# A two-layer adaLN transformer on one core: another order of the tail, and an earlier modulate in layer 0

## The chip, the cores and the metric

The kernel runs on 1 core of one Trainium2 chip. The metric is device time in microseconds (us) of one execution. Three executions of the kernel before the change took 626.12, 626.17 and 625.37 us: median 626.12. Durations in this document that belong to single instructions come from the profile of one more execution of the same kernel.

A core has five engines, each with its own instruction stream, run strictly in the order in which the kernel writes it: TensorE (PE in the profile; its weight loads are listed as PEld), VectorE (DVE), ScalarE (ACT), GpSimd (POOL) and SyncE (SP), which here only issues DMAs. Engines wait for one another by semaphores.

## The reference: what is computed

Tokens x of shape 8 x 256 x 128 pass through two layers. Each layer is an attention block and a mixture-of-experts block, each with a layernorm in front that is scaled and shifted by vectors worked out from a condition c, and each added back to x with a gate:

```python
h = _layernorm(x, axis=-1) * (1 + ca) + sa
x = x + ga * attention(h)
h = _layernorm(x, axis=-1) * (1 + cb) + sb
x = x + gb * ffn(h)
```

Layer 0: 16 heads of width 8, causal; then 8 experts with a hidden width of 512, top 2 by softmax, plus a shared expert. Layer 1: 16 heads of width 64, causal; then 16 experts with a hidden width of 64 (silu(x wg) * (x wu), times wd), top 2 by sigmoid, plus a shared expert, plus the block's own input.

## The kernel before the change

All of it is in float32. The 2048 tokens lie in four wide tiles of 512 (x[0] to x[3]; a wide tile is two batches of 256, or four token tiles of 128). The change touches `fast_path` only. (The program ends by reading a flag, `bad`, which sends unusual inputs to another path; with these inputs that path isn't taken.)

From the end of layer 0's first layernorm on, the schedule is manual: each engine's order is exactly the order in which the Python code writes the steps.

**Layer 0's attention** is a loop over 24 units (three per batch, line 1427). Unit n issues, in this order: scores0 (TensorE scores, ScalarE exponentials, GpSimd masks), in every third unit the projections of the next batch (project0, L1101, L1104 and L1106), then the list `early[n]` (filled by `at`), then values0 of unit n-2 (L1162), project_v0, and then the list `ends[n]` (filled by `at_end`). Layernorm of wide tile w is cut into `measure`, `normalise` and `modulate`. `modulate` is four transposes on TensorE (L771) and two VectorE writes of h (L774). Wide tile w is measured at the end of unit 6w-6, normalised in 6w-5, and modulated in 6w-3; the projection in unit 6w-2 is the first to read its h. Also in the lists around there: `finish0` (TensorE y L1198, VectorE t L1200 and x L1201), the second layernorm (`norm0`: statistics L746 and L748, xn0b L762), and `gates0` (L1256 to L1261).

**Layer 1's experts.** Wide tiles 0 to 2 are routed sparsely: their tokens were scattered by expert into `xs` in DRAM, in tiles of 128 rows, and ten groups m = 0 to 9 of four tiles each are worked through by

- `fetch_weights1(m)` (m from 4 on, L1760 and L1764): SyncE reads four expert numbers into registers and issues four DMAs of 128 KB. Each group has a buffer of its own or one that is long free.
- `fetch_rows1(m)` (L1742, L1035): four DMAs of 64 KB from `xs`; called by `turn1(m - 4)`.
- `turn1(m)`: four transposes (L1779), a ScalarE copy to xTs (L1781), and `fetch_rows1(m + 4)`.
- `hidden1(m)`: 16 matmuls (L1790), ScalarE silu (L1795), VectorE product (L1796).
- `project_tiles(m)`: 8 matmuls (L1803), two VectorE copies into `ysb` (L1809; three buffers, each free when its DMA has landed), and the DMA of `ysb` to `ys` in DRAM (L1810, 256 KB).

When all of `ys` has landed, `gather1(j)` for the 12 token tiles fetches each token's two rows back (L1047, 24 indirect DMAs on GpSimd). `combine1(j)` weighs and adds them (ScalarE L1912, VectorE L1913); at each wide tile's end it multiplies by the gate and adds to x (L1916, L1917: on GpSimd for wide tiles 0 and 1, on VectorE for 2) and issues the output. The buffers of its sums are shared with the token tiles of `norms`, two in all, so wide tile 1's combine waits for norms[1]'s last step on GpSimd and wide tile 2's for wide tile 0's.

Wide tile 3 is computed densely: `finish1` of the last batch, the layernorm of that batch (`norms[1][0]` measure, `[1]` normalise, `[2]` modulate, `[3]` tokens and `[4]` add, the last two on GpSimd), the router (`go7`, four steps; `go6` is the same for the batch before), `gate_rows(k)` (a transpose, a VectorE copy gT L1829, and DMAs through DRAM into `gp`, L1830 and L1837), `dense_hidden(p)` for 8 pairs of experts (TensorE L1852, ScalarE silu L1846, VectorE product L1847), `dense_gate(p)` (VectorE, times `gp`, L1857) and `dense_project(p)` (TensorE L1862). `shared_hidden`, `shared_project` and `ffn1_add` do the shared expert of two wide tiles, and the final adds (L1894, L1895). `spread_last` (L1648, L1652) and `reciprocals1` belong to the last batch's attention; `tables` is 18 VectorE instructions that make the gather's indices; `flag` reduces the judgement (L1923), adds it up on TensorE and writes `bad` (L1927).

The order of all this after the attention loop is one written list of some 105 calls (from line 2018). The lines that matter most, with their numbers:

```python
    at_end(n + 3, modulate)                        # 1398, in the loop over w
    fetch_weights1(8)                              # 2030
    fetch_weights1(9)                              # 2031
    hidden1(9)                                     # 2059
    for j in range(TT * LAST): gather1(j)          # 2064
```

Of the kernel before, what the change touches and what calls it, by code (L numbers as in the profile page):

```python
# [17 lines left out]
B, S = 8, 256  # L18
# [539 lines left out]
def fast_path(ctx: ExitStack, tc: tile.TileContext, i: dict, out: bass.AP, bad: bass.AP):  # L558
# [819 lines left out]
    def at_end(n, *steps):  # L1378
        ends.setdefault(n, []).extend(steps)
# [13 lines left out]
    for w in range(1, NW):  # L1393
        measure, normalise, modulate = layernorm_parts(w, md[0], SA, CA, f"0a{w}", ps_ln)
        n = 6 * w - 6
        at_end(n, measure)
        at(n + 1, normalise)
        at_end(n + 3, modulate)
        at_head(n + 2, 1, lambda w=w: add_bias(w))
    for b in range(B - 1):  # L1400
        at_end(3 * b + 4, lambda b=b: normalise0(b))
# [194 lines left out]
    def values1(b, u):  # L1596
        v = st1["v", b, u // 2]
        if u == 0:
            st1["s", b] = pp.tile([P, S], F32, tag="sum", bufs=1, name=f"sum1_{b}")
            st1["ou", b] = lp.tile([P, 2, 4, S], F32, tag="ou", name=f"ou1_{b}")  # L1600
        s = st1["s", b]
        o = pp.tile([P, 2, S], F32, tag="o", bufs=1, name=f"o1_{b}_{u}")
        pts = [st1.pop(("pt", b, 2 * u + m)) for m in range(2)]
        for m in range(2):
            for kb, cols, qs in blocks:
                for n in range(2):
                    nc.tensor.matmul(  # L1607
                        out=o[bass.ts(n, D1), m, qs], lhsT=v[:, kb, bass.ts(4 * (u % 2) + 2 * m + n, D1)],
                        rhs=pts[m][:, n, cols], start=(kb == 0), stop=(kb == 1), skip_group_check=True,
                    )  # L1610

        for kb, cols, qs in blocks:
            for m in range(2):
                for n in range(2):
                    nc.tensor.matmul(  # L1615
                        out=s[bass.ts(2 * n + m, 32), qs], lhsT=on[:, u, :], rhs=pts[m][:, n, cols],
                        start=(kb == 0 and u == 0), stop=(kb == 1 and u == 3), skip_group_check=True,
                    )
        nc.vector.tensor_copy(st1["ou", b][:, :, u, :], o)

    def reciprocals1(b):
        r = st1["r", b] = lp.tile([P, S], F32, tag="r", name=f"r1_{b}")
# [12 lines left out]
        st1["rb", b] = rb  # L1635
        judge(r)
# [138 lines left out]
    def turn1(m):  # L1775
        xT_ps = ps_ln([P, 4, P], f"xT1_{m}")
        xg = sq.pop(("x", m))
        for t in range(4):
            nc.tensor.transpose(xT_ps[:, t, :], xg[:, t, :], ident)  # L1779
        xT = sq["xT", m] = lp.tile([P, 4, P], F32, tag="xT", name=f"xTs1_{m}")  # L1780
        nc.scalar.copy(xT, xT_ps)  # L1781
        if m + 4 < NQ:
            fetch_rows1(m + 4)

    def hidden1(m):
        xT = sq.pop(("xT", m))
# [229 lines left out]
    norms = [norm1((b, 1)) for b in (B - 2, B - 1)]  # L2016
    go6, go7 = (one(route1((b, 1))) for b in (B - 2, B - 1))
    values1(*divmod(N - 1, 4))
    reciprocals1(B - 1)
    turn1(0)  # L2020
    hidden1(0)
    turn1(1)
    turn1(2)
    hidden1(1)
    add()
    project_tiles(0)
    fetch_weights1(7)
    turn1(3)
    project_tiles(1)
    fetch_weights1(8)  # L2030
    fetch_weights1(9)
    hidden1(2)
    turn1(4)
    tables()
    hidden1(3)
    norms[0][0]()
    project_tiles(2)
    turn1(5)
    norms[0][1]()
    hidden1(4)  # L2040
    project_tiles(3)
    turn1(6)
    hidden1(5)
    norms[0][2]()
    project_tiles(4)
    turn1(7)
    hidden1(6)
    hidden1(7)
    norms[0][3]()
    project_tiles(5)  # L2050
    go6()
    turn1(8)
    norms[0][4]()
    project_tiles(6)
    turn1(9)
    go6()
    hidden1(8)
    project_tiles(7)
    hidden1(9)
    go6()  # L2060
    project_tiles(8)
    spread_last()
    project_tiles(9)
    for j in range(TT * LAST): gather1(j)
    shared_hidden(0)
    go6()
    finish1(B - 1)
    norms[1][0]()
    gate_rows(0)
    norms[1][1]()  # L2070
    norms[1][2]()
    norms[1][3]()
    shared_project(0)
    go7()
    shared_hidden(2)
    go7()
    dense_hidden(0)
    go7()
    dense_hidden(1)
    go7()  # L2080
    shared_project(2)
    ffn1_add(0)
    dense_hidden(2)
    dense_hidden(3)
    gate_rows(1)
    ffn1_add(1)
    ffn1_add(2)
    dense_hidden(4)
    dense_hidden(5)
    judge(st1["r", B - 1])  # L2090
    norms[1][4]()
    judged = flag()
    next(judged)
    dense_hidden(6)
    dense_gate(0)
    dense_gate(1)
    dense_hidden(7)
    combine1(0)
    dense_gate(2)
    dense_project(0)  # L2100
    combine1(1)
    dense_project(1)
    dense_gate(3)
    dense_project(2)
    dense_project(3)
    combine1(2)
    combine1(3)
    dense_gate(4)
    combine1(4)
    dense_gate(5)  # L2110
    dense_gate(6)
    dense_project(4)
    combine1(5)
    combine1(6)
    combine1(7)
    dense_gate(7)
    dense_project(5)
    combine1(8)
    combine1(9)
    dense_project(6)  # L2120
    dense_project(7)
    combine1(10)
    combine1(11)
    ffn1_add(LAST)
    next(judged, None)
    nc.sync.dma_start(out=out[:, bass.ts(LAST, TT), :], in_=x[LAST])
    manual.close()
    l1.close()

# [93 lines left out]
```

## Time and profile before

| what | us |
|---|---|
| median of three executions | 626.12 |
| the profiled execution | 627.05 |
| its span | 625.2 |
| TensorE busy over the span | 545.0 (87%) |
| VectorE busy | 351.0 (56%) |
| GpSimd busy | 301.8 (48%) |
| ScalarE busy | 274.5 (44%) |
| granted TensorE clock, mean | 0.942 |

The profiled execution lies 1.85 us above its own span, and 0.93 us above the median of the three. "Busy" on TensorE counts pipelined matmuls with modelled ends. The granted clock is the share of TensorE's full speed that it was given: the same hidden1 group of 16 matmuls takes 1.09 us at 1.00 and 1.98 us at 0.50.

Landmarks of the profiled execution, in us from the start of the span: layer 0's attention runs from about 20 to 130; layer 1's attention ends at 525; groups 0 to 9 run from 526.02 (first transpose) to 565.49 (last matmul of group 9); gathers run from 569.52 to 599.34; the last VectorE instruction ends at 615.2.

### The profile page before, as it was taken

What the parts mean: (1) busy time and instruction counts of PE and PEld (TensorE: products, weight loads), DVE (VectorE), ACT (ScalarE), POOL (GpSimd) and SP (SyncE); (2) the same over time, 40 slices, a digit from 0 to 9 for tenths busy, and PEclk for the clock granted to TensorE, in tenths of its full rate; (3) what the DMA queues carried; (4) which work ended last, traced back from release to release, by engine and by line L of the source; (5) the groups of instructions that cost most, each with busy time, mean ns of one, the idle gap of its engine ahead of it and who ended that gap; (6) DMA issues with size and microseconds to landing.
All of it is one profiled execution on the core that took longest, in us unless ns stands there. A gap on an engine that the chain in (4) does not pass through costs nothing.

```text
span 625.2 us, 11930 instructions
## 1 busy us (share of the span) xinstructions
PE 545.0 (87%) x4391; PEld 386.4 (62%) x4391; DVE 351.0 (56%) x1069; ACT 274.5 (44%) x486; POOL 301.8 (48%) x456
## 2 busy tenths in 40 slices
PE   3699879878899899789999999999999998888960
PEld 3344435445699899656676767657676766665350
DVE  3448897875632222246536556574838384644793
ACT  1476465736145455345534363435353532433230
POOL 7356586857404443238532056543446543104771
PEclk9899797979989999979999999999999999879996
DMA  8999990131239999131030203030303036653541
GB/s 277 339 408 403 389 331 9 38 112 34 62 100 285 313 316 308 36 151 35 19 85 10 61 17 88 30 72 2 78 14 87 14 78 186 172 159 77 115 98 56
DMA packets 52911, 85.41 MB, mean 137 GB/s; under 512 B 6428, under 2 KB 32156, under 8 KB 51692
## 3 DMA queue, kind: packets, MB, share of 16 engines
q1 hardware_dynamic: 44444, 59.77, 30.0%
q0 software_dynamic: 8400, 24.78, 12.8%
q8 instruction: 37, 0.61, 0.4%
q14 instruction: 30, 0.25, 0.1%
HBM read 53.46 MB, written 31.07 MB: 135 GB/s over the span
## 4 chain that ended last, share of the span: by engine, by line
PE 61%; DVE 15%; DMA 7%; POOL 5%; ACT 4%; issue 4%; SPq 1%; DVEq 0%; POOLq 0%; ACTq 0%
PE sc L1585 7%; PE o L1607 6%; PE qp L1554 5%; PE hp L1338 5%; PE yt L1346 5%; PE vp L1567 5%; PE kp L1554 4%; PE y L1660 4%; POOL yg L1047 3%; PE sum L1615 3%; PE sc L1137 3%; PE o L1162 2%; DMA wt<-in_wpk_dram,widx 2%; PE hp L1272 2%; PE qk L1101 1%
## 5 line engine op out<-in xcount | busy, mean ns | idle before, releaser
L812 POOL TENSOR_SCALAR_AFFINE_SELECT pt<-pt 128x256 f32<-128x256 f32 (+1 forms) x176 | 89.3, 533 | 112.1 <-ACT pt L1588 79.6
L1047 POOL DMA_INDIRECT yg<-ys,yidx x56 | 53.9, 962 | 52.1 <-DMA ys<-ysb 33.9
L1588 ACT ACTIVATE pt<-sc 128x768 f32<-128x768 f32 x64 | 48.4, 808 | 25.5 <-PE sc L1585 25.4
L1141 ACT ACTIVATE pt<-sc 128x1024 f32<-128x1024 f32 x48 | 46.5, 1023 | 16.7 <-PE sc L1137 16.3
L1039 POOL DMA_INDIRECT wt<-in_wpk_dram,widx x31 | 29.2, 942 | 50.1 <-PE xT L1329 48.6
L1340 ACT ACTIVATE hst<-hp,wt 128x128 f32<-128x128 f32 x136 | 38.9, 368 | 30.4 <-ACT hst L1340 20.5
L1585 PEld LDWEIGHTS sc<-q,k 64*128 64x128 f32 x512 | 41.6, 187 | 16.4 <-issue 11.5
L1585 PE MATMUL sc<-q,k 64*128 64x256 f32 (+1 forms) x512 | 50.5, 336 | 0.0
L1607 PE MATMUL o<-pt,v 128*64 128x256 f32 (+1 forms) x512 | 48.7, 332 | 1.8 <-POOL pt L812 1.8
L1570 ACT COPY v<-vp 128x512 f32<-128x512 f32 x32 | 18.8, 586 | 67.6 <-PE vp L1567 56.7
L1350 DVE COPY ysb<-yt 128x128 f32<-128x128 f32 x39 | 11.4, 291 | 58.5 <-PE yt L1346 58.5
L1607 PEld LDWEIGHTS o<-pt,v 128*64 128x64 f32 x512 | 31.8, 136 | 19.7 <-POOL pt L812 5.6
L1558 DVE COPY q<-qp 128x512 f32<-128x512 f32 x32 | 22.0, 688 | 38.8 <-PE qp L1554 38.8
L1137 PE MATMUL sc<-qm,k 32*128 32x512 f32 x192 | 37.7, 716 | 5.3 <-ACT pt L1141 4.4
L1338 PE MATMUL hp<-xTs,wt 128*128 128x128 f32 x272 | 36.5, 277 | 3.2 <-DMA wt<-in_wpk_dram,widx 2.4
L1554 PE MATMUL qp<-h,wq 128*128 128x256 f32 x128 | 37.1, 413 | 1.3 <-DVE sh L1299 1.3
L924 POOL DMA_INDIRECT xs<-ht0b,idx x32 | 31.7, 990 | 13.5 <-issue 4.8
L1567 PE MATMUL vp<-wv,h 128*128 128x512 f32 x64 | 36.0, 645 | 1.1 <-DVE q L1558 1.1
L1338 PEld LDWEIGHTS hp<-xTs,wt 128*128 128x128 f32 x272 | 33.0, 192 | 4.7 <-issue 3.3
L1346 PE MATMUL yt<-wt,hst 128*128 128x128 f32 x272 | 35.8, 275 | 0.0
L1558 ACT COPY k<-kp 128x512 f32<-128x512 f32 x32 | 18.8, 588 | 35.7 <-PE kp L1554 35.6
L1554 PE MATMUL kp<-h,wk 128*128 128x256 f32 x128 | 33.7, 387 | 0.0
(296 smaller groups left out, 1138.5 us busy)
## 6 DMA issues: line engine op xcount, KB each, us to landing
xs<-zero SPq DMA_DIRECT2D x1, 12288.0 KB
xs<-zero SPq DMA_DIRECT2D x1, 8192.0 KB
rb<-rd SPq DMA_DIRECT2D x14, 512.0 KB, 6.1
mdb<-mrd SPq DMA_DIRECT2D x2, 2048.0 KB
xg<-xs SPq DMA_DIRECT2D x63, 64.0 KB, 2.0
wt<-in_wpk_dram SPq DMA_DIRECT2D x24, 128.0 KB, 2.1
wst<-in_wpk_dram SPq DMA_DIRECT2D x5, 514.0 KB, 12.6
ys<-ysb SPq DMA_DIRECT2D x10, 256.0 KB, 4.7
```

Source lines behind the costliest of these rows:

```text
L812: nc.gpsimd.affine_select(out=pt, in_=pt, compare_op=ALU.is_ge, fill=0.0, base=0, pattern=[[0, pt.shape[1]], [1, P]], channel_multiplier=-1,)
L1047: nc.gpsimd.indirect_dma_start(out=yg[:, k, :], out_offset=None, in_=self.ys[:, :], in_offset=bass.IndirectOffsetOnAxis(ap=self.yidx[:, j, ...
L1137: nc.tensor.matmul(out=sc[:, n, :].rearrange("p (a q) -> p a q", q=rhs.shape[2]), lhsT=k[r, cols], rhs=rhs, start=True, stop=True,)
L1141: nc.scalar.activation(pt[:, bass.ts(half, 2), :], sc, AF.Exp)
L1338: nc.tensor.matmul(out=hp[:, c, :], lhsT=wt[:, bass.ts(c, P)], rhs=xT, start=True, stop=True)
L1346: nc.tensor.matmul(out=y, lhsT=hs[:, c, :], rhs=wt[:, bass.ds(WF + c * P, P)], start=(c == 0), stop=(c == FC - 1))
L1554: nc.tensor.matmul(out=ps_[:, n, :], lhsT=w1[f"w{what}1"][:, bass.ts(2 * u + n, P)], rhs=hb, start=True, stop=True)
L1558: copy(st1[what, b, u], ps_)
L1567: nc.tensor.matmul(out=vp, lhsT=hb[:, bass.ts(j, P)], rhs=w1["wv1"][:, bass.ts(half, 512)], start=True, stop=True)
L1585: nc.tensor.matmul(out=sc[:, n, cols], lhsT=k[r, m, bass.ts(kb, P)], rhs=q[r, m, qs], start=True, stop=True)
L1588: nc.scalar.activation(pt, sc[:, :, 0:384], AF.Exp, scale=1.0 / math.sqrt(D1))
L1607: nc.tensor.matmul(out=o[bass.ts(n, D1), m, qs], lhsT=v[:, kb, bass.ts(4 * (u % 2) + 2 * m + n, D1)], rhs=pts[m][:, n, cols], start=(kb == ...
```

## The change

Part 1, layer 0: `modulate` of wide tiles 1 to 3 goes from the end of its unit to the list `early` of the same unit, and stands first in it. It thus runs after that unit's scores and before its values, half a unit sooner.

Part 2, the tail: the same calls in another order. No call is added or removed, and no function is changed. In words: two turns come before the first hidden; fetch_weights1(9) moves from behind fetch_weights1(8) to behind hidden1(7), and so behind the DMAs of project_tiles(2) to (5); hidden1(4) and turn1(6) come one place sooner, project_tiles(4) comes before hidden1(5), project_tiles(5) before hidden1(6); a routing step (`go6`) comes sooner; finish1 of the last batch goes before shared_hidden(0) and the gathers; shared_hidden(2) goes before the router's first step, shared_project(2) before the dense products; the adds (`ffn1_add`), gates, projections and combines of the dense part are interleaved differently; the flag's reduction moves behind combine1(7), and the last output's DMA ahead of the flag's last step.

```diff
-        at_end(n + 3, modulate)
+        at(n + 3, modulate)
...
     values1(*divmod(N - 1, 4))
+    turn1(0)
     reciprocals1(B - 1)
-    turn1(0)
+    turn1(1)
     hidden1(0)
-    turn1(1)
+    hidden1(1)
     turn1(2)
-    hidden1(1)
     add()
     project_tiles(0)
     fetch_weights1(7)
     turn1(3)
     project_tiles(1)
     fetch_weights1(8)
-    fetch_weights1(9)
     hidden1(2)
     turn1(4)
     tables()
     hidden1(3)
     norms[0][0]()
     project_tiles(2)
+    hidden1(4)
     turn1(5)
     norms[0][1]()
-    hidden1(4)
+    turn1(6)
     project_tiles(3)
-    turn1(6)
-    hidden1(5)
     norms[0][2]()
     project_tiles(4)
+    hidden1(5)
+    go6()
     turn1(7)
+    project_tiles(5)
     hidden1(6)
     hidden1(7)
+    fetch_weights1(9)
     norms[0][3]()
-    project_tiles(5)
     go6()
+    norms[0][4]()
     turn1(8)
-    norms[0][4]()
     project_tiles(6)
+    hidden1(8)
     turn1(9)
+    project_tiles(7)
     go6()
-    hidden1(8)
-    project_tiles(7)
     hidden1(9)
-    go6()
     project_tiles(8)
     spread_last()
     project_tiles(9)
+    finish1(B - 1)
+    go6()
+    norms[1][0]()
     for j in range(TT * LAST): gather1(j)
     shared_hidden(0)
-    go6()
-    finish1(B - 1)
-    norms[1][0]()
     gate_rows(0)
     norms[1][1]()
     norms[1][2]()
+    shared_hidden(2)
     norms[1][3]()
+    go7()
+    go7()
     shared_project(0)
-    go7()
-    shared_hidden(2)
+    shared_project(2)
     go7()
     dense_hidden(0)
-    go7()
+    ffn1_add(0)
     dense_hidden(1)
     go7()
-    shared_project(2)
-    ffn1_add(0)
     dense_hidden(2)
+    norms[1][4]()
+    ffn1_add(1)
     dense_hidden(3)
     gate_rows(1)
-    ffn1_add(1)
-    ffn1_add(2)
     dense_hidden(4)
     dense_hidden(5)
+    ffn1_add(2)
     judge(st1["r", B - 1])
-    norms[1][4]()
-    judged = flag()
-    next(judged)
-    dense_hidden(6)
     dense_gate(0)
     dense_gate(1)
+    judged = flag()
+    dense_hidden(6)
     dense_hidden(7)
+    dense_project(0)
+    dense_gate(2)
+    dense_gate(3)
+    dense_project(1)
+    dense_project(2)
     combine1(0)
...
     combine1(7)
-    dense_gate(7)
+    next(judged)
+    dense_project(4)
+    combine1(8)
...
     ffn1_add(LAST)
+    nc.sync.dma_start(out=out[:, bass.ts(LAST, TT), :], in_=x[LAST])
     next(judged, None)
-    nc.sync.dma_start(out=out[:, bass.ts(LAST, TT), :], in_=x[LAST])
```

More of the change, by code (lines that the diff above doesn't have):

```diff
@@ L2071, in fast_path @@
     norms[1][2]()
+    shared_hidden(2)
     norms[1][3]()
+    go7()
+    go7()
     shared_project(0)
-    go7()
-    shared_hidden(2)
+    shared_project(2)
     go7()
     dense_hidden(0)
-    go7()
+    ffn1_add(0)
     dense_hidden(1)
     go7()
-    shared_project(2)
-    ffn1_add(0)
     dense_hidden(2)
+    norms[1][4]()
+    ffn1_add(1)
     dense_hidden(3)
     gate_rows(1)
-    ffn1_add(1)
-    ffn1_add(2)
     dense_hidden(4)
     dense_hidden(5)
+    ffn1_add(2)
     judge(st1["r", B - 1])
-    norms[1][4]()
-    judged = flag()
-    next(judged)
-    dense_hidden(6)
     dense_gate(0)
     dense_gate(1)
+    judged = flag()
+    dense_hidden(6)
     dense_hidden(7)
+    dense_project(0)
[3 more added lines that the diff above has]
+    dense_project(2)
     combine1(0)
-    dense_gate(2)
-    dense_project(0)
+    dense_project(3)
     combine1(1)
[L2102 to L2105, printed above, removed]
     combine1(2)
+    dense_gate(4)
     combine1(3)
-    dense_gate(4)
+    dense_gate(5)
     combine1(4)
-    dense_gate(5)
     dense_gate(6)
-    dense_project(4)
+    dense_gate(7)
     combine1(5)
@@ L2115, in fast_path @@
     combine1(7)
-    dense_gate(7)
+    next(judged)
+    dense_project(4)
+    combine1(8)
     dense_project(5)
-    combine1(8)
+    dense_project(6)
     combine1(9)
-    dense_project(6)
+    combine1(10)
     dense_project(7)
-    combine1(10)
     combine1(11)
     ffn1_add(LAST)
+    nc.sync.dma_start(out=out[:, bass.ts(LAST, TT), :], in_=x[LAST])
     next(judged, None)
-    nc.sync.dma_start(out=out[:, bass.ts(LAST, TT), :], in_=x[LAST])
     manual.close()
```

## The prediction

> **What bounds the kernel now.** I read the page first: no engine is full over the span (PE, the busiest, 87%), so the stages were read one by one. Then the chain that ended last, from 526 us on (start us, us, what):
>
> ```profile
> 547.51 0.33 SPq L1035
> ...
> 549.49 2.49 DMA ys<-ysb
> 551.99 0.02 issue
> 552.01 0.44 DVE ysb L1809
> 552.45 0.14 issue
> 552.58 0.55 PE yq_o L1803
> ...
> 566.31 2.27 DMA ys<-ysb
> ```
>
> From 542.55 to 549.49 the chain runs through SyncE's queue (SPq), which issues DMAs one after the other. Its own timeline shows what stood in it:
>
> ```profile
> 541.58 0.38 SPq L1810 DMA_DIRECT2D ys<-ysb  x1
> 542.55 4.72 SPq L1764 DMA_DIRECT2D wt<-in_wpk_dram  x8
> 547.51 1.88 SPq L1035 DMA_DIRECT2D xg<-xs  x4
> 549.49 0.38 SPq L1810 DMA_DIRECT2D ys<-ysb  x1
> 550.12 1.92 SPq L1035 DMA_DIRECT2D xg<-xs  x4
> ```
>
> The x8 are the weights of tile groups 8 and 9, issued together. Behind them wait the rows of group 8, the results (`ys`) of group 2, whose landing frees the buffer that VectorE needs for group 5's results at 552.01, and the rows of group 9. TensorE then pays twice: it idles (2.70 of 4.50 us busy, columns: stretch, length, PE busy), and the next stretch runs at a granted clock of 0.58 (column after the five engines):
>
> ```profile
> 549.50:554.00 4.50, 2.70 (x12) 1.81 (x12) 0.85 (x3) 1.50 (x3) 0.00 (x0) 0.80 0.72 202
> 554.00:560.00 6.00, 6.00 (x51) 4.91 (x52) 3.51 (x13) 2.54 (x4) 0.00 (x0) 0.58 0.50 138
> ```
>
> The last `ys` lands at 568.58; GpSimd then needs 24 gathers at 1.25 us (0.95 and 0.30 of issue), 569.52 to 599.34. But the tail is not GpSimd's alone. VectorE's timeline from 597 on:
>
> ```profile
> 597.13 1.34 DVE L1857 TENSOR_TENSOR a<-a,gp 128x512 f32<-128x512 f32 x2 [0.89 <-DMA gp<-gd]
> ```
>
> VectorE waits for the gate rows `gp`, then works to 615.1 almost without a gap (15.11 us busy of the 16 from 600): gates and combines end the kernel together with GpSimd. From 615.1 to 625.2 only the last output, the flag and the end remain, and the change leaves them.
>
> **Part 1, layer 0.** For wide tiles 1, 2, 3 the four transposes (0.66 us) and two writes of h (0.96 to 0.99) move ahead of the values step of units 3, 9, 15. Nothing is added; no DMA is moved.
> - Tile 1: TensorE runs without a gap from the scores (35.23) to the projection (39.86). Order changes, the sum doesn't: 0.
> - Tile 2: the transposes fill a wait of TensorE for `aT` (0.84 us), but h goes ahead of `t`, `x` and the statistics. `aT` ends 57.42, h would run to 58.4, `t` could have begun at 58.22: +0.2 on the chain through the layernorm.
> - Tile 3: TensorE waits for h (0.96 us, last bracket):
>
> ```profile
> 92.72 2.07 PE L1101 MATMUL qk<-h,wqkv 128*128 128x256 f32 x4 [3.51 <-DVE h L774]
> ```
>
> VectorE is the bound here (gates 85.71 to 90.38). h now stands before `t`, `x`, statistics instead of after: it starts at 90.38, not 92.15, and the projection 1.8 us sooner; but the statistics, ScalarE's root and `xn0b` follow, `xn0b` 0.2 later, so the next transposes, which were held by the projection until 94.58, now by `xn0b`, gain only about 0.4.
> Sum -0.2; bounds -1.0 (all of tile 3's slack reaches the end) and +0.9 (0.97 us of h before the statistics, nothing saved).
>
> **Part 2, to project_tiles(9).** The instructions are the same but for one table load (below). What counts:
> - fetch_weights1(9) leaves its place behind group 8 and goes behind project_tiles(5). Group 9's share of the x8 is 547.51 - 544.88 = 2.6 us (4 DMAs of 0.52 and the register loads). Without it: rows of group 8 from 544.74, `ys` of group 2 issued 546.7 and landed (2.49 as above) 549.2, rows of group 9 to 549.3, `ys` of groups 3, 4, 5 at 549.4, 549.9, 550.3. VectorE gets the buffer at 549.2, not 552.01.
> - The start is denser: two turns before the first hidden fill the 0.68 and 0.24 us waits for ScalarE's copies, hidden1(4) and turn1(6) run while VectorE does tables (534.95 to 538.94). By project_tiles(3) this is worth some 1.2 us, but it then runs into the queue above: project_tiles(4) and (5) outrun `ys` 1 (landing 544.0) and 2 (549.2), and VectorE, in order, holds group 6's product and the routing steps behind them. So the gain here is the queue's, not the sum.
> - From 549.2: copies 0.76, two products 0.84: project 6 at 550.5 (now 552.58). Five pieces at full clock (project 0.72, hidden 1.09, turn 0.66, project 0.72) bring TensorE to 553.9, ready for hidden 9.
> - The new wait: group 9's weights. They stand behind `ys` 5 (550.3), so DMAs from 551.2 to 552.8; landing 2.1 after issue (median of the 24 rows): 554.9. hidden 9 waits 1.0 us; behind it on TensorE stand projects 8 and 9 and spread_last, and for them the last `ys` and all gathers. Project 8 starts at about 555.7, now 559.59; from there to the end of project 9 nothing changes (5.9 us). **Gain 3.9.** Bounds of the landing: 2.1 (nearest row, same DMA) and 6.1 (`gp` rows, queue full): 0 to 4.0 less gain.
>
> One rule bears on the clock. In the trace, half clock follows gaps of 2.2 us (538.0, then 0.50 at 542 to 544) and even of 1.0 to 1.5 (62 to 64, 70 to 72, then 0.53 to 0.59), while gaps of 1.0 to 1.3 at 588 and 596 cost nothing. The Trainium skill, "TensorE: Matmul & The Clock Gate", "What's actually happening", gives an idle window of about 3.4 us before half rate; by it the gaps of 0.4 to 1.5 us left here would be free and the gain stays 3.9. The rows are less kind. At half clock for one such stretch (554 to 560 held 3 us of full-rate work) the gain falls by up to 1.9. I take full clock, as the gaps are shorter than the two that cost most.
>
> **Part 2, after project_tiles(9)**, as offsets from its end (565.49 now). finish1 goes ahead of shared_hidden(0): `y` ends 1.8 sooner, but the silu before the root now waits for shared_hidden(0), and the next transposes stay at about +8.5 (now +8.34). shared_hidden(2) goes ahead of the router: its silu, the exponential, silu again: one table load more.
> ScalarE's loads take 1.283 us each here, with the next activation 0.01 behind; this one lies beside TensorE's hidden work, cost 0 (bound 1.3). The Trainium skill, "ScalarE: Activation LUTs", "What ACT_TABLE_LOAD costs", says some 2.66 us per switch, which would add at most 2.7; no row here has the second half of that.
> VectorE decides what follows:
> - ffn1_add(1) (1.37) now stands before the copy of gate_rows(1); the routing starts 0.4 sooner: `gp` lands at +32.7, now +31.64: **+1.0**.
> - dense_gate(0) and (1) stand before the product of dense_hidden(6), which ran under the wait for `gp` at 595.55: **+0.7**.
> - The flag's reduction (0.42), at 595.22 under the same wait, moves behind combine1(7): **+0.4**.
> - The other gates, combines and adds change places among themselves: 0. The gathers move past finish1, one routing step and a measure, none of which is on GpSimd: 0. reciprocals1 (1.76 us, VectorE) and turn1(0) swap on different engines, and the last output's DMA passes the flag's last step on SyncE's queue only, issued at 615.12 with x ready at 615.10: 0. GpSimd's order (gathers, tokens, add, two combines) stays. combine1(3) comes some 1.8 us later for GpSimd's pass over wide tile 0, but VectorE still has work until combine1(8), so this is covered; without that cover up to 1.1 more, a combine beside GpSimd taking 1.35 where it takes 0.34 alone.
> **Given back 2.1**; bounds 0 (the gathers alone decide) and 3.2.
>
> **Sum.** -0.2 - 3.9 + 2.1 = -2.0. The profiled execution took 627.05 (span 625.2, 1.85 around it): 625.05. The median shown, 626.12, is 0.93 lower: 624.1.
>
> **Rivals.**
> - Gathers decide (tail gives back nothing): 626.1 - 4.1 = 622.0, and 620.6 if group 9's weights are also in time (1.0) with the denser start adding some 0.4. For it: ScalarE's combines waited 4.31 and 3.29 us for GpSimd. Against: VectorE's full 16 us.
> - Half clock in the stretch: gain 2.0, -0.2 - 2.0 + 2.1: 626.0, no change. For it: the gaps of 1.45 us before 550.5.
> - Slower: group 9's weights come late. Place: hidden 9; price: each us after 553.9 goes to the gathers one to one. Landing as `gp` (6.1 after issue, beside three `ys` of 256 KB): 558.9, gain -0.1, total +2.0: 628.1. It turns slower when they land over 2.0 us behind the forecast (past 556.9). Against: in this trace three `ys` together moved in some 3 us at 300 GB/s.
> - The queue isn't the bound, and the chain's link is a coincidence: gain 0.5 to 1, 627.0.
>
> **How the numbers follow.** 0.2% (1.25 us) is about what measurement tells from no change here: faster is under 624.87, slower over 627.37. Forecast 0.40 (own range 622.9 to 625.3: 0.34 faster, 0.06 same); gathers decide 0.22 (faster); half clock 0.20 (0.02, 0.16, 0.02); late weights 0.13 (0, 0.02, 0.11); queue not the bound 0.05 (0, 0.02, 0.03). Faster 0.58, same 0.26, slower 0.16. The range leaves out the far ends of the gathers case and half of the late weights: 620.6 to 627.6.
>
> **What would show it.** Right: the SyncE timeline has four weight DMAs, not eight, before group 8's rows; VectorE's wait for `ys` ends near 549; the first gather starts near 565.6; `gp` lands some 33 us after project 9. Wrong: hidden 9 waits over 2 us for `wt`; the clock falls under 0.6 in 552 to 560; the first gather moves by under 2 us; or the projection at 92.7 stays.

## The result, and the profile after

The changed kernel takes 628.98 us (median of 20 executions, 624.08 to 633.18); the kernel before, on the same chip, 625.88 (20 executions, 622.01 to 629.27). The ratio is 1.0073, with a 95% interval of 1.0054 to 1.0093: slower by some 4.6 us. All ratios and intervals here are those recorded with the runs, in which executions over 1.5% above the fastest of the same kernel are left out; they need not equal the quotient of the medians, which are of all executions (here 1.0050, or 3.1 us). Forecast were 624.1 us and a range up to 627.6, so sign and range are both wrong.

The one profile of the changed kernel hides this: its execution took 626.82 us, 0.23 less than the profiled one of before, and its span is 625.1 us against 625.2. That time is the lowest but one of the twenty. The profile is read for mechanisms only; what each part costs comes from the timed runs below.

**The queue did what was forecast.** SyncE's timeline of the changed kernel:

```profile
544.00 1.95 SPq L1764 DMA_DIRECT2D wt<-in_wpk_dram  x4
546.50 1.89 SPq L1035 DMA_DIRECT2D xg<-xs  x4
548.49 0.38 SPq L1810 DMA_DIRECT2D ys<-ysb  x1
...
553.82 2.24 SPq L1764 DMA_DIRECT2D wt<-in_wpk_dram  x4
```

Four weight DMAs stand ahead of group 8's rows, not eight, and group 9's follow behind the rows of group 9 and the results of groups 3 to 5. The chain of waits then runs through those late weights (start us, us, what):

```profile
548.49 2.48 DMA ys<-ysb
551.06 0.65 DVE ysb L1809 x2
...
553.82 3.26 DMA wt<-in_wpk_dram
557.22 1.88 PE gu L1790 x16
```

Here everything upstream lies 1.2 us later than in the profile of before (first transpose 527.20, not 526.02). Counted from the first transpose, VectorE's copies for group 5 start at 23.9 us (before: 26.0; forecast 23.2), hidden 9 at 30.0 (before 32.1; forecast 28.9), and project 9 ends at 37.0 (before 39.5; forecast 35.6). The late weights are not all of it: TensorE itself is ready for hidden 9 only at 29.9 (forecast 27.9) and waits 0.2 us for them. The first gather starts at 568.21, 1.3 us sooner than before in the clock of the profile and 2.5 sooner counted from the first transpose; the prediction had named less than 2 us as a sign of being wrong.

**Behind project 9** the gates came late, as forecast. VectorE's timeline after:

```profile
597.57 2.01 DVE L1857 TENSOR_TENSOR a<-a,gp 128x512 f32<-128x512 f32 x2 [1.37 <-DMA gp<-gd]
```

From the end of project 9 (564.22) that is 33.35 us, before 31.64, so 1.7 later where 1.0 was forecast; VectorE's last large instruction ends 1.6 later, counted the same way. Forecast were 2.1: the moved gates and the flag, priced at 1.1 together, added nothing here. The added table load lies on the chain to `gp`. ScalarE's timeline:

```profile
578.22 1.28 ACT L1712 ACT_TABLE_LOAD   x1
579.51 0.23 ACT L1712 ACTIVATE p<-p 128x32 f32<-128x32 f32 x1
```

This exponential of the router waits 0.5 us for the load (VectorE had its input ready at 579.02). It starts 15.3 us after project 9, where it started 10.8 after it; the prediction had the routing 0.4 sooner.

**Layer 0** ran ahead and lost it again. Unit 16's scores start 2.3 us sooner than before (85.77, was 88.07), unit 23's 1.4 later (127.08, was 125.72). The stretches between, cut where the granted clock changes (columns: stretch, length, busy us of PE, PEld, DVE, ACT and POOL, then PEclk, DMA share, GB/s):

```profile
85.80:89.20 3.40, 1.11 (x12) 0.28 (x8) 3.26 (x7) 0.37 (x1) 3.05 (x4) 1.00 1.02 397
89.20:92.60 3.40, 2.04 (x4) 1.18 (x4) 3.23 (x16) 0.79 (x2) 2.16 (x3) 0.50 0.88 355
92.60:96.00 3.40, 3.17 (x37) 2.33 (x38) 2.24 (x7) 3.39 (x5) 1.33 (x2) 0.50 0.02 8
96.00:99.40 3.40, 2.34 (x21) 1.74 (x21) 2.70 (x11) 1.16 (x3) 3.30 (x4) 1.00 0.08 24
99.40:102.80 3.40, 3.28 (x22) 1.10 (x20) 2.87 (x12) 1.93 (x3) 0.82 (x2) 0.50 0.00 0
102.80:106.30 3.50, 3.50 (x16) 1.60 (x16) 2.21 (x8) 2.06 (x3) 2.24 (x7) 0.50 0.00 0
106.30:109.70 3.40, 3.40 (x26) 1.08 (x22) 2.34 (x8) 0.00 (x0) 1.56 (x3) 0.50 0.00 0
```

The granted clock changes only at whole steps of 3.41 us, called windows below; a half window is one at 0.50. Five of these seven are at 0.50; in the profile of before, three in the same place.

### The profile page after: what moved, and what is told of

Same layout as the page of the kernel before. It is cut to its first block, busy times and chain, and to the rows that moved or that the text cites. A ratio compares the mean times of both kernels' runs of the same rounds, so it can differ in the third digit from the quotient of the medians.

```text
span 625.1 us, 11934 instructions
## 1 busy us (share of the span) xinstructions
PE 548.0 (88%) x4391; PEld 387.4 (62%) x4391; DVE 351.6 (56%) x1069; ACT 275.4 (44%) x487; POOL 300.8 (48%) x456
## 3 DMA queue, kind: packets, MB, share of 16 engines
q1 hardware_dynamic: 44444, 59.77, 29.9%
## 4 chain that ended last, share of the span: by engine, by line
PE 63%; DVE 17%; DMA 6%; ACT 5%; POOL 3%; issue 3%; SPq 1%; DVEq 0%; POOLq 0%; ACTq 0%
PE sc L1585 7%; PE o L1607 6%; PE hp L1338 6%; PE qp L1554 5%; PE yt L1346 5%; PE y L1660 5%; PE vp L1567 5%; PE kp L1554 4%; PE sc L1137 3%; PE sum L1615 3%; PE o L1162 2%; PE hp L1272 1%; PE qk L1101 1%; DMA bout<-in_bout_dram 1%; DMA wt<-in_wpk_dram,widx 1%
## 5 line engine op out<-in xcount | busy, mean ns | idle before, releaser
L812 POOL TENSOR_SCALAR_AFFINE_SELECT pt<-pt 128x256 f32<-128x256 f32 (+1 forms) x176 | 89.4, 534 | 111.5 <-ACT pt L1588 79.5
L1137 PE MATMUL sc<-qm,k 32*128 32x512 f32 x192 | 39.4, 745 | 5.0 <-ACT pt L1141 4.1
L1558 DVE COPY q<-qp 128x512 f32<-128x512 f32 x32 | 22.0, 688 | 38.7 <-PE qp L1554 38.7
## 6 DMA issues: line engine op xcount, KB each, us to landing
xs<-zero SPq DMA_DIRECT2D x1, 8192.0 KB, 26.8
```

Of the source, the lines that this page charges most:

```text
L812: nc.gpsimd.affine_select(out=pt, in_=pt, compare_op=ALU.is_ge, fill=0.0, base=0, pattern=[[0, pt.shape[1]], [1, P]], channel_multiplier=-1,)
L1137: nc.tensor.matmul(out=sc[:, n, :].rearrange("p (a q) -> p a q", q=rhs.shape[2]), lhsT=k[r, cols], rhs=rhs, start=True, stop=True,)
L1558: copy(st1[what, b, u], ps_)
```

## The experiments

Each kernel was timed in turn with the kernel before on the same chip (the kernel before itself ran once). The chips differ: on some the kernel before takes 624 us, on others 643 to 644. So only ratios are compared, and every ratio below is to the kernel before on its own chip.

| kernel | median us | before us | ratio | 95% interval |
|---|---|---|---|---|
| part 1 only | 647.08 | 643.22 | 1.0033 | 1.0000 to 1.0066 |
| part 2 (tail) only | 645.62 | 643.22 | 1.0042 | 1.0012 to 1.0072 |
| before, weights of group 9 back | 642.09 | 643.22 | 0.9954 | 0.9915 to 0.9993 |
| the changed kernel again | 650.30 | 643.22 | 1.0091 | 1.0051 to 1.0132 |
| tail up to project 9 only | 642.30 | 643.36 | 0.9970 | 0.9939 to 1.0001 |
| tail behind project 9 only | 646.06 | 643.36 | 1.0039 | 1.0006 to 1.0073 |
| part 1, tile 3 only | 645.55 | 643.36 | 1.0014 | 0.9984 to 1.0045 |

**Which part loses?** Theory A: layer 0 (its order moves the stretches at half clock). Theory B: the tail, in executions that were not profiled. Theory C: both.

Part 1 alone:

```diff
-        at_end(n + 3, modulate)
+        at(n + 3, modulate)
```

> The kernel before with part 1 alone (transposes and h of wide tiles 1 to 3 in the first half of their units); the tail is as before. In the two profiles layer 0 ran up to 1.9 us ahead until unit 17, then went at half clock between 100 and 110 us, and from there to layer 1's end the changed kernel lay 1.2 to 1.4 us behind. Theory A (layer 0 makes the loss: its order moves the stretches at half clock): 1.003 to 1.009 of the time before, some 628 to 631 us. Theory B (the tail makes the loss): 0.997 to 1.001, some 624.5 to 626.5. Theory C (both, each with a part): about 1.002 to 1.004.

The changed kernel with that line undone (the tail alone):

```diff
-        at(n + 3, modulate)
+        at_end(n + 3, modulate)
```

> The changed kernel with part 1 undone: only the tail in the other order. In the one profile the tail up to the last matmul of group 9 was 1.3 us ahead and gave 1.9 back behind it. Theory A (layer 0 makes the loss): 0.996 to 1.000, some 623.5 to 626. Theory B (the tail loses in executions that were not profiled, by weights of group 9 that land late or by gates that wait longer): 1.005 to 1.009, some 629 to 631. Theory C: about 1.002 to 1.004.

The kernel before with one line moved:

```diff
     fetch_weights1(8)
-    fetch_weights1(9)
...
     hidden1(7)
+    fetch_weights1(9)
```

> The kernel before with one line moved: fetch_weights1(9) goes from behind fetch_weights1(8) to behind hidden1(7), and so out of the queue ahead of the rows of groups 8 and 9 and of the results of group 2. Everything else is as before. If SyncE's queue is what held VectorE until 552.01 us, as the prediction has it, the buffer comes free at some 549.2 us, the first gather starts 2 to 3 us sooner and nothing behind it gives time back: 0.995 to 0.997, some 623 to 624 us. If the queue is not the bound, or the late weights of group 9 take its place: 0.999 to 1.003.

The changed kernel, unaltered:

> The changed kernel once more, for another profile of it. Its times so far lie in two heaps, around 627.3 and around 631.8 us, and the profile seen is of the lower one. If this profile is of the upper heap it shows where the 4.5 us are lost: theory A, as more time at half clock in layer 0 or 1, ahead of 526 us; theory B, behind 526 us. The ratio again 1.005 to 1.009.

Measured 1.0033, 1.0042, 0.9954 and 1.0091. By these values both halves lose, as theory C has it, and the whole exceeds the sum of its halves by 0.16%, well inside the intervals. Part 1's interval begins at 1.0000, so its time alone doesn't exclude theory B. The moved weights alone gain 3.0 us by the ratio, 1.1 by the medians. Their profile shows the mechanism more than the size: VectorE's copies for group 5 start 24.1 us after the first transpose (25.2 to 26.6 in the five profiles of the old front without filler), so the queue was a bound, as the prediction said; but project 9 ends at 37.8 (38.0 to 39.5) and the first gather starts at 41.9 (42.0 to 43.5), 0.2 to 1.6 sooner and not 2 to 3.

The changed kernel's eleven times fall into two groups again, 645.6 to 647.1 (five) and 650.3 to 654.7 (six), and its profile, at 646.98, is of the lower one, as the first was. Where the upper group loses its further 4 to 5 us, no profile shows.

**Where in the tail, and which tile in layer 0?** The tail's list was cut at project_tiles(9), with the new order on one side and the old on the other.

> The kernel before with the tail's new order up to project_tiles(9) alone; layer 0 and all behind project_tiles(9) as before. The prediction put a gain of 3.9 us here. The whole tail measured 1.004 of the time before, and moving fetch_weights1(9) alone 0.995. If the loss of the tail lies behind project_tiles(9): 0.994 to 0.997 here. If it lies in the rest of the front's order (the denser start, hidden 9 waiting for its weights), so that only the moved weights are worth anything: 0.999 to 1.004.

> The kernel before with the tail's new order behind project_tiles(9) alone. The prediction put 2.1 us of loss here: 1.003. If the loss of the tail lies here and is larger than forecast: 1.006 to 1.010. If the tail's loss lies in its front: 1.000 to 1.004.

The kernel before, unaltered, for a profile:

> The kernel before, for a profile on the chip that the other kernels of this call run on. In the last four profiles ScalarE and TensorE stood still for up to 21 us while GpSimd's 24 gathers ran, and the span was 17 to 20 us longer than in the first two profiles. If that is the chip's doing and not the changes', this profile shows the same, with a span about as long as that of the other kernels of this call.

Tile 3 alone:

```diff
-        at_end(n + 3, modulate)
+        (at if w == 3 else at_end)(n + 3, modulate)
```

> The kernel before with part 1 for wide tile 3 alone (unit 15). In the profiles its h comes 1.8 to 3 us sooner, TensorE then stands idle in two pieces around 85 to 92 us, and four windows of 3.4 us at half clock follow where the kernel before has two or three. If tile 3 makes part 1's loss: 1.002 to 1.006. If tiles 1 and 2 make it (order of VectorE around 57 us): 0.998 to 1.000, since tile 3 alone was forecast to gain 0.4 us.

Measured 0.9970, 1.0039 and 1.0014; the kernel before took 640.85 us in its one execution. The front gains 1.9 us (0 to 3.9), the back loses 2.5 (0.4 to 4.7): close to the 2.1 of the prediction, and less than the larger loss that the theories allowed for. Together that is +0.6 us, while the whole tail alone measured +2.7 (0.8 to 4.6) on another chip; the intervals overlap, but the pieces don't account for the tail's loss. Tile 3 alone is not told apart from no change by its time, but its profile has the whole pattern of part 1 (below).

The profile of the kernel before shows where the chips at 643 us lose: ScalarE stands still while GpSimd's gathers run (565.90 to 595.63), with the kernel unaltered (in brackets the idle time and what the profile puts its end down to; it names nothing that ScalarE waited for):

```profile
592.00 0.60 ACT L1846 ACTIVATE a<-gud 128x512 f32<-128x512 f32 x1 [8.49 <-issue]
599.73 1.08 ACT L1846 ACTIVATE a<-gud 128x512 f32<-128x512 f32 x2 [7.13 <-remote]
```

On the first chip these waits were 1.1 to 2.8 us. So the difference belongs to the chip, and the changes are judged by ratios alone. It also means that the back was timed where other waits decide. In the profile of the tail behind project 9 alone, ScalarE stands still once, for 21 us:

```profile
599.48 1.09 ACT L1846 ACTIVATE a<-gud 128x512 f32<-128x512 f32 x2 [21.03 <-remote]
```

There VectorE's gates start at 615.40 without any wait for `gp`. So the 2.5 us there are not the late gate rows that the prediction priced.

**Is the half clock what part 1 costs?** Start of unit 16's, 17's and 23's scores, of the sorted experts' first and last hidden matmul, and of the tail's first transpose; mean and range over the profiles without filler in layer 0 (nine without part 1, four with it or its tile 3):

| | 16 | 17 | 23 | first hp | last hp | tail | half windows, 85 to 110 us |
|---|---|---|---|---|---|---|---|
| without | 86.0 | 98.3 | 123.6 (121.7 to 125.7) | 172.0 | 250.3 | 524.5 (522.1 to 526.2) | 2 to 3, once 4 |
| with | 85.1 | 98.6 | 125.4 (124.6 to 127.1) | 173.3 | 253.4 | 528.1 (526.8 to 530.0) | 4 to 5 |

The early h gains 0.9 us up to unit 16; by unit 23 the kernel is 1.9 us behind, by the tail 3.6. In the profile of the tail's front alone (without part 1) TensorE's idle time lies in one window and its work behind it is dense, so full clock comes back after one:

```profile
87.00:90.50 3.50, 0.32 (x1) 0.30 (x2) 3.43 (x14) 0.75 (x2) 3.12 (x5) 0.99 1.02 412
90.50:93.90 3.40, 3.40 (x28) 2.16 (x30) 3.07 (x11) 3.39 (x5) 2.69 (x4) 0.51 0.53 210
93.90:97.30 3.40, 2.67 (x37) 2.10 (x33) 2.28 (x12) 1.21 (x3) 3.31 (x4) 1.00 0.06 19
```

In all four profiles with part 1 the projection comes early and leaves a second wait behind it, here in the second profile of the changed kernel (before: one wait of 3.51 us):

```profile
88.44 1.10 PE L1101 MATMUL qk<-h,wqkv 128*128 128x256 f32 x4 [2.28 <-issue]
91.52 1.23 PE L771 MATMUL nt0b<-ident,xn0b 128*128 128x128 f32 x4 [1.97 <-DVE xn0b L762]
```

In the profile of tile 3 alone three windows in a row lack work for it, and four run at half:

```profile
86.80:90.20 3.40, 1.10 (x4) 0.68 (x4) 3.33 (x15) 0.02 (x1) 3.02 (x5) 1.00 1.03 415
90.20:93.60 3.40, 2.10 (x24) 1.52 (x28) 3.07 (x10) 3.37 (x4) 2.01 (x3) 0.50 0.53 210
93.60:97.00 3.40, 2.35 (x25) 1.66 (x18) 1.38 (x10) 1.95 (x5) 3.21 (x4) 0.50 0.06 19
97.00:100.40 3.40, 3.40 (x17) 2.19 (x16) 2.84 (x12) 0.23 (x1) 0.90 (x1) 0.50 0.02 5
100.40:103.80 3.40, 3.40 (x26) 1.39 (x24) 2.45 (x8) 1.94 (x2) 1.83 (x2) 0.50 0.00 0
```

From unit 17 to 23 the four profiles with part 1 take 26.3 to 28.4 us, eight of the nine without 25.0 to 25.3. The ninth (the tail's front with early weights, below) has layer 0's old order, but four half windows by chance of where they fell, and takes 26.4. So these 1.1 us seem to go with the clock and not with the order itself, as far as one profile can tell.

The next kernels fill TensorE's waits with work that changes nothing. First by issuing scores again:

```diff
-                nc.tensor.matmul(
+                for _ in range(1 + half * {16: 5, 22: 4}.get(3 * b + u, 0)):
+                    nc.tensor.matmul(
```

> The kernel before, with work added that changes nothing: in units 16 and 22 of layer 0 the last two score matmuls are issued again (5 and 4 times, into the same PSUM tile, about 0.57 us each time), in stretches where TensorE stands idle for 2.7 to 3.5 us and ScalarE's exponentials wait for its root anyway. Theory clock (a window of 3.4 us in which TensorE has little to do is paid for with one to four windows at half clock): the half windows at 90 to 103 and 117 to 124 us go, the expert stage of layer 0 starts 2 to 5 us sooner, 0.992 to 0.998. Theory order (layer 0 is set by VectorE's chain, and the clock only fills in its waits): 1.000 to 1.003.

On part 1, with {16: 3, 22: 4}:

> Part 1 alone with the same kind of filler (unit 16 three times, for its gap is 2.3 us there, unit 22 four times). Theory clock (part 1 loses because the early h splits one idle stretch of TensorE in two and makes four half windows of two): the loss goes, and this kernel is as fast as the kernel before with filler, within 0.2%; 0.992 to 0.998. Theory order (part 1 loses by what VectorE does later because of h): about 0.3% slower than the kernel before with filler, 1.000 to 1.004.

Measured 1.0200 (1.0162 to 1.0237) and 1.0125 (1.0079 to 1.0171): both theories missed, because the filler was too long. TensorE's timeline of the first:

```profile
84.98 12.07 PE L1138 MATMUL sc<-qm,k 32*128 32x512 f32 x28
```

Eight records on four groups of 32 rows take 1.14 us side by side; 20 more, group by group, took 10.9, and the 12 more on part 1 took 4.5. Nor did this filler hold the clock. A wholly busy window of the first kernel is followed by half:

```profile
87.30:90.70 3.40, 3.40 (x13) 1.75 (x12) 3.33 (x15) 1.42 (x2) 3.02 (x5) 1.00 1.03 418
90.70:94.10 3.40, 3.40 (x5) 1.33 (x4) 1.25 (x6) 1.19 (x2) 2.51 (x3) 0.50 0.38 147
```

On part 1 only that one half window followed, and in spite of the filler's length unit 17 started at 97.1 us (98.3 to 98.7 without) and 22 at 114.4 (115.7 to 118.6 without), as in the kernels without part 1 (96.7 to 100.6 and 113.8 to 117.2); in unit 22 the filler then cost more than that. This is the best sign for the clock, from one profile.

Smaller, in unit 16 alone: {16: 1} on part 1, and {16: 2} on the kernel before.

> Part 1 alone, with the last two score matmuls of unit 16 issued twice (1.5 us by the 0.37 us that each of the four records took in the too long filler, in a wait of 2.3 us). Theory clock: unit 17 starts at 96.5 to 97.5 us, where part 1 without filler has 98.3 to 98.7, and one or two half windows follow instead of four; part 1's loss goes, 0.997 to 1.001. Theory order: 98.3 to 98.7 us as without filler, 1.002 to 1.005.

> The kernel before, with the last two score matmuls of unit 16 issued three times (3.0 us in a wait of 3.5). The control to the part 1 kernel with filler. Theory clock: unit 17 starts 0.5 to 1.5 us sooner than the 96.7 to 98.8 us without filler; 0.997 to 1.000. Theory order: as without filler or up to 0.5 us later; 1.000 to 1.002.

Measured 1.0093 (1.0072 to 1.0114) and 1.0032 (1.0013 to 1.0050), on a chip where the kernel before takes 624.36. Four half windows stayed on part 1, and unit 17 started at 99.6; on the kernel before there were two, and unit 17 started at 97.1, no sooner than the earliest without filler. Both speak for theory order, or for a filler that was too weak: on part 1 it took 0.9 us, not the 1.5 planned. Part 1 with this small filler alone loses 5.8 us there, at least as much as the whole change on the first chip. Last, with matmuls over the whole array (twice in unit 16 on part 1; three times there and twice in unit 22 on the kernel before):

```diff
+            for _ in range(half * {16: 2}.get(3 * b + u, 0)):
+                nc.tensor.matmul(out=sc[:, 0, :], lhsT=ident, rhs=h[0], start=True, stop=True)
             for n in range(2):
```

> Part 1 alone, with two matmuls over the whole array (128 rows, 512 columns, 1.0 us each by the row of L1852, where two records take 1.02) ahead of the last scores of unit 16, in a wait of 2.3 us; their result is overwritten. In 18 profiles a window of 3.4 us in which TensorE was busy under 0.4 was always followed by half clock (80 of 80), one busy 0.8 or more never, except behind the fillers that use 32 of the array's 128 rows. Theory clock: the window at 86 to 90 us is then over 0.8 busy, no half window follows in 89 to 97 us, unit 17 starts at 96.5 to 97.5 us (98.3 to 99.6 without), 23 at 122 to 123 (124.6 to 127.1 without), 0.997 to 1.002 where part 1 had 1.003. Theory order: 98.3 to 99.5 us and 1.003 to 1.008.

> The kernel before with the same filler, three times in unit 16 (3.1 us in a wait of 3.5) and twice in unit 22 (2.0 us in 2.7). Theory clock: the half windows at 89 to 103 and at 117 to 126 us go or become fewer (one instead of two or three at each place), 23 starts at 121 to 122.5 us and the expert stage 2 to 4 us sooner; 0.994 to 0.998, faster than both kernels. Theory order, or if the filler stands in the way where the clock is half: 1.000 to 1.004.

Measured 1.0059 (1.0025 to 1.0093) and 1.0062 (1.0030 to 1.0095). On part 1 only one half window went (the one at 89); the one at 92.6 and three from 99 on stayed, and units 17 and 23 started at 98.6 and 127.0, as in the changed kernel. The test did not take the half clock away, so it doesn't tell the theories apart. On the kernel before the filler did hold the clock (85.20 to 102.30 at 1.00, one half window behind), unit 17 started at 96.7 and 23 at 122.7, among the early ones; but unit 17 to 22 took 18.3 us, more than in any of the nine (16.6 to 17.8), so fewer half windows alone don't make the stretch short. And the kernel is slower: in its profile the experts took 82.5 us from first to last hp (76.7 to 79.5 in the nine profiles of the table without part 1), with two waits for weights of 1.8 and 2.0 us. Part 1 alone shows the same kind of wait (1.9 us, stage 82.4). What makes them come is open.

**What holds the front?** Either the half clock or group 9's weights. The front with a filler over the whole array:

```diff
-        for t in range(4):
-            nc.tensor.transpose(xT_ps[:, t, :], xg[:, t, :], ident)
+        for t in range(12 if m == 6 else 4):
+            nc.tensor.transpose(xT_ps[:, t % 4, :], xg[:, t % 4, :], ident)
```

> The tail's new front alone (0.997 measured), with the four transposes of turn1(6) issued three times over, 1.3 us more of TensorE's time in the wait before project_tiles(3). In all four profiles of the new front three full windows at half clock follow that wait, 14 to 25 us after the first transpose; in the old front one or two, with less work in them. Theory clock: they go, the stretch from the first transpose to the end of project_tiles(9) falls from 37.0 us to 34 to 35.5, 0.990 to 0.994. If the queue and VectorE set the stretch and the half clock lies in their waits: 37 us as without filler, 0.996 to 0.998.

Measured 0.9982 (0.9948 to 1.0016). In the front alone, three windows at half clock follow the wait:

```profile
534.20:537.60 3.40, 1.93 (x16) 1.30 (x12) 3.23 (x15) 2.91 (x5) 0.00 (x0) 1.00 0.68 183
537.60:541.00 3.40, 3.40 (x23) 2.62 (x24) 2.07 (x7) 1.40 (x2) 2.18 (x3) 0.50 0.69 196
```

With the filler that place is at full clock (first transpose at 525.1), but two half windows come later, from 549.5 to 556.3:

```profile
539.30:542.70 3.40, 3.16 (x34) 2.43 (x32) 2.04 (x7) 1.46 (x2) 2.13 (x3) 1.00 0.71 201
...
549.50:552.90 3.40, 2.87 (x24) 2.50 (x24) 3.09 (x13) 0.00 (x0) 0.00 (x0) 0.50 0.79 216
```

The stretch to project 9 still takes 37.6 us, not less than without (36.8 to 37.0 in three of the four profiles of the new front, 38.7 in the fourth). Up to VectorE's copies for group 5 the clock is not the bound: they start 23.8 us after the first transpose, 23.3 to 24.0 without filler, and TensorE at full clock only waited longer. Behind them the test decides nothing, for the filler moved the half windows into that place: from the copies to the end of its work before hidden 9 TensorE takes 6.5 us, 5.2 to 7.3 without filler.

Both fillers of the first kind with the front:

> The tail's new front with both fillers, layer 0 and what lies behind project_tiles(9) as before. Theory clock: the sum of the gains, 0.983 to 0.992. If only the front's order is worth something: 0.996 to 0.999.

1.0161 (1.0123 to 1.0199); the scores' filler again.

Weights of group 9 early:

```diff
-          lambda: fetch_weights1(6))
+          lambda: fetch_weights1(9), lambda: fetch_weights1(6))
...
-    fetch_weights1(9)
```

> The kernel before with fetch_weights1(9) alone moved, this time forward: into unit 30 of layer 1's attention, ahead of fetch_weights1(6), where SyncE waits 2.7 us for a buffer (522.4 to 525.1 us). The queue behind it is then 2.6 us shorter, as with the weights moved back, and group 9's weights can't be late. If the queue held the old front as the prediction had it: from the first transpose to the end of project_tiles(9) 35 to 36.5 us where the old front has 38.0 to 39.5; 0.993 to 0.996. If something else took its place (VectorE, the clock): 37.5 to 38.5 us, 0.998 to 1.001.

> The tail's new front alone, with fetch_weights1(9) in unit 30 as well. In the new front hidden 9 waits for its weights until 30.0 to 30.6 us after the first transpose; TensorE was forecast ready at 27.9. If these late weights are what the front's gain fell short by: the stretch falls from 37.0 to 34.5 to 35.5 us, 0.990 to 0.994. If the half windows set it: 36.5 to 37.5 us, 0.996 to 0.999.

Measured 0.9993 (0.9976 to 1.0009) and 0.9988 (0.9967 to 1.0010). SyncE's timeline of the first shows that the free place was not there:

```profile
523.77 4.46 SPq L1764 DMA_DIRECT2D wt<-in_wpk_dram  x8
528.47 6.88 SPq L1035 DMA_DIRECT2D xg<-xs  x12
```

The weights did not go out during the wait but together with group 6's, and the rows of groups 4 to 6 start 6.4 us after the first transpose instead of 3.4. The queue was moved, not shortened: the copies for group 5 start 26.4 us after the first transpose (26.8 with the new front), as before (26.0). With the new front hidden 9 no longer waits for weights, but starts only at 31.4. So the times of these two don't answer whether late weights are what the front lacks; that the queue sets the start of the copies they agree with. The second profile shows one thing more: between the copies and hidden 9 there is no half window, and TensorE is ready for hidden 9 after 4.7 us, just what the prediction forecast (549.2 to 553.9).

## Why the prediction was wrong, step by step

- **Part 1, "Sum -0.2; bounds -1.0 and +0.9": wrong. Here, and in the next point, are the steps that failed.** Measured +2.1 us (0 to 4.2) alone. Each order of VectorE that it describes came true: h and the projection of tile 3 come sooner (88.58 and 89.71, were 92.15 and 92.72). Of h's 3.6 us, 1.7 come from upstream: counted from the end of the gates, h starts 1.8 us sooner, as forecast, xn0b 0.5 later (forecast 0.2) and the transposes behind it no sooner (forecast 0.4). What failed is the bound: it priced instructions only. It put at nothing that TensorE's idle time, cut into two waits, is followed by more windows at half clock. Shown: four or five half windows in 85 to 110 us in all four profiles with part 1, and 1.0 us or more from unit 17 to 23 wherever four or five are. Not shown: that the clock is all of it. Between unit 23 and the tail another 1.7 us are lost, and the only filler that freed part 1 from most of its half windows cost more elsewhere.
- **Part 2 to project_tiles(9), "Gain 3.9": right on the queue, half the size.** Measured 1.9 (0 to 3.9), and 3.0 (0.5 to 5.5) for the moved line alone. The buffer comes free 2.1 us sooner, as worked out to 0.7. The terms that failed stand behind it. "Five pieces at full clock" were to take TensorE 4.7 us to hidden 9; in the four profiles of the new front they took 5.2 to 7.3, so it was ready at 29.2 to 30.6 us after the first transpose, not 27.9. The weights are issued later than assumed and land 3.3 us after, not 2.1. Hidden 9, forecast at 28.9, starts at 30.0 to 30.6: in two of the four profiles it waits 0.8 and 1.2 us for weights, in the others 0 and 0.2. Either term alone would have held it near 30. (Small slips in the sum: four pieces are priced where five are named, and weights at 554.9 with a hidden of 1.09 put project 8 at 556.0, not 555.7.) And the profile of before was a slow draw: its front takes 39.5 us, the old front in four other profiles 38.0 to 38.9.
- **The rival "Half clock in the stretch"** came true as an event (three windows in each of the four profiles of the new front), and in part as a cost. The two with 2.3 and 2.6 us of half clock between the copies and hidden 9 took 6.0 and 7.3 us there, the two with 0.5 us or less took 5.2 and 5.3, and the one without any (weights early) 4.7. In the profile of the tail alone one more half window, 31.0 to 34.4 us after the first transpose, falls on hidden 9 and project 8, and project 9 ends at 38.7, 1.7 to 2.0 later than in the other three. What the clock costs on the mean is not shown.
- **Behind project_tiles(9), "Given back 2.1": right in size, in part by luck.** 2.5 us (0.4 to 4.7) in time, but on a chip where VectorE doesn't wait for `gp`; 1.6 in the pair of profiles, where `gp` came 1.7 later (forecast 1.0) and the gates and the flag, forecast at 1.1, added nothing.
- **The extra table load, "cost 0", and "the routing starts 0.4 sooner": wrong**, in the one profile of the pair. The load holds the router's exponential by 0.5 us, and with shared_hidden(2) now ahead of the router that exponential comes 4.5 us later, counted from project 9. Of this 1.7 reach `gp`.
- **The slower rival** ("group 9's weights come late", past 556.9) is not what made it slower: they landed at 557.1 here, 555.9 without the 1.2 us from upstream. (The three `ys` ahead of them moved at 250 to 280 GB/s in the profile of before, not 300.)

By these parts the change is +2.1 - 1.9 + 2.5 = +2.7 us. The whole measured +4.6 (3.4 to 5.8) on the first chip and +5.9 (3.3 to 8.5) on the second. The difference is within the sum of the intervals; whether the parts add up is not settled. Both profiles of the changed kernel come from its lower times, so what is lost on top in the higher ones stays open.

The version to keep is the kernel before with fetch_weights1(9) behind hidden1(7), nothing else: 0.9954 (0.9915 to 0.9993), measured on a chip of 643 us only, and 1.1 us by the medians.

## What to carry to other kernels

Reorder one thing at a time: here one moved line held the gain, and the edits around it lost more, by their mean values. Moving a matmul into the middle of a wait did not shorten the wait here, and spread it over more clock windows, so count windows as well as microseconds. And take bounds from several profiles: the one used here was the latest of nine at unit 23 of layer 0 and the slowest of the five old fronts without filler.

## What the runs showed of the hardware

- **One slack window is enough for half clock.** Busy share here is the time with a matmul under way in each 3.41 us window, cut where the granted clock steps, over 20 profiles, from 25 to 560 us. A full-clock window under 0.4 busy was followed by half clock 87 times of 87; from 0.4 to 0.5, 16 of 28; from 0.5 to 0.8, 39 of 233; from 0.8 on, 6 of 2468, all six behind the fillers on one group of 32 rows. Half clock ended 147 times, always after a window at least 0.9 busy; but 46 half windows at least as busy as those were followed by another. The Trainium skill, "TensorE: Matmul & The Clock Gate", "What's actually happening", has the free-running window of 3413 ns, with which these runs agree, and puts half rate after an idle window; here a window that was up to 0.4 busy was enough, without exception.
- **Where the grid falls is chance.** Windows start at another place of the program in each execution (in the profiles of before and after, 91.4 and 89.2 us), and the same order of layer 0 (nine profiles, on several chips) ran unit 23 anywhere from 121.7 to 125.7 us. That spread is as large as the effects sought.
- **Matmuls on different groups of 32 rows ran side by side, those on one group one after the other**: 0.14 us a record when four groups run side by side, against 0.37 (12 in 4.5 us) to 0.55 (20 in 10.9 us, in part at half clock) in the long fillers. The fillers' repeats also write one and the same place in PSUM; which of the two keeps them apart no run here shows.
- **Chips differ by 19 us** on the same kernel (624.36 and 643.36), in ScalarE's and TensorE's waits while the gathers run. What they wait for the profile does not name.
